# A selective-scan and attention kernel: the C-row product and the state sums of a group placed after the slot's other TensorE work, and y copied and gated one slot later

## The chip, the cores and the metric

One core of one Trainium2 chip. The metric is the device time of one execution in microseconds (us). The engines are named as the profile names them: PE (TensorE matmuls; PEld is its weight loads), DVE (VectorE), ACT (ScalarE), POOL (GpSimd) and SP (SyncE, which issues most DMAs). Each engine works through its own queue in the order in which the kernel's instructions were written down; between engines, semaphores hold an instruction back until what it needs is there.

## The reference

The input x is 4 batches of 512 channels on 64 x 64 positions (4096 tokens a batch), float32. Two residual layers follow each other, each on a group-normed input:

```python
x = x + mamba_layer(group_norm(x))       # layer 0
x = x + linear_attention(group_norm(x))  # layer 1
```

Layer 0 normalizes each token, cuts the 512 channels into 4 chunks of 128 and runs the same selective scan on each chunk, then a norm and a 512 x 512 projection. In a chunk, 128 channels are projected to xi and z of 256 channels each; xi goes through a causal convolution of 4 taps and silu to give xc; from xc come dt (256 channels), B and C (16 states each per token). Then, token after token:

```python
dA = exp(dt_t[:, :, None] * A)                       # 256 channels x 16 states
h  = dA * h + (dt_t * x_t)[:, :, None] * B_t[:, None, :]
y  = einsum('bds,bs->bd', h, C_t)                    # sum over the 16 states
...
y  = (y + xc * D_param) * silu(z)
out = einsum('bld,od->blo', y, out_proj_w)
```

Layer 1 is a linear attention with 8 heads: q, k through relu, k^T q summed over all tokens of a batch, normalized, and then applied to v and the output projection. Its work needs all tokens of layer 0 of a batch, and runs beside layer 0 of the next batch.

## The kernel before

**Tiling.** A step is one batch b, one tile t of 512 tokens and one chunk c of 128 channels: 4 x 8 x 4 = 128 steps. A step has 256 inner channels in two halves e of 128, and 16 states in four quarters q of 4. A pair (e, q) is a *group*: its tile h is 128 x 4 x 512, where the partition holds 4 states x 32 channels and the middle index j one of four blocks of 32 channels. So there are 8 groups a step and 1024 in all. A group takes two *slots* (jj = 0 and 1), each with two of the four j: 16 slots a step, 2048 in all. In what follows an even slot has jj == 0 and an odd slot jj == 1.

**One slot** (`slot`, line 725) writes down, in this order:

- POOL: `drive(g + 2)` (line 717), the product bx = (dt x) B for the slot after next (3 buffers);
- SP: the loads of a row of B (even slots) or of the last 128 columns of C (odd slots), each broadcast over partitions;
- DVE: the first scan (line 739) of 512 tokens, h[j] = dA h + bx, from a dA in PSUM and a bx in SBUF. ACT: the `decay` of number k + 3 (line 708), dA = exp(dt A), into one of three PSUM banks, so it follows scan k;
- in an even slot only, between the first and the second scan, for the group that ended in the slot before: `product(g - 1)` (line 756), in which DVE multiplies the first 384 columns of h by C, read from the PSUM tile c_all; and `fold_states(g - 1)` (line 761), all on PE: `c_row` (line 702) makes the next c_all by a matmul with a selection matrix, at q == 0 four small matmuls put xc D into the y bank (`diagonal`, line 128), and four matmuls with `fold` sum the states of h into y;
- the second scan and its decay;
- in an odd slot, POOL: the last state of each channel is copied to `st`, and the last 128 columns of h are multiplied by C (line 751);
- `after()` (line 1108), everything else.

The tiles h have two buffers, so the first scan of an even slot overwrites the h of the group before last, and waits until its four fold matmuls are done. The c_all tile and the y tile have one bank each. Three more PSUM banks (`ps_w`) serve all other matmuls in turn.

**The rest of the work.** `after()` runs in each slot s = 0..15 of a step n. First the things that are due: a matmul result written to a `ps_w` bank in one slot is copied out, mostly by ACT, one slot later (`later`, line 86). Then, by slot number: `take_y` (line 777), in which ACT copies y from PSUM to SBUF once a half is summed up; `spread` (line 633), 8 DMA issues on SP that load dt and dt x of the next half; `gate` (line 780), in which POOL multiplies y by silu(z); the time steps of step n + 1 (matmuls in slot 2, ACT in slot 3); `out_proj` of step n - 1 in slot 4 (four matmuls on the input, then two on the gated y); the input projection with its convolution for step n + 2 (`inputs`, line 579, `pc` and `pz` banks) in slots 3 to 9; silu in slot 10; the projections to dt, B and C (`mixers`, line 642) from slot 12 on. Last, a planner takes pieces of three queues (the norm of the next tile, the output of a finished tile, the attention of a finished batch) as long as a credit of 3.5 matmuls of 512 columns a slot allows. What has been written down since the slot before, folds included, is charged to that credit.

After the last step, the attention of the last batch runs alone.

Of the kernel before, what the change touches and what calls it, by code (L numbers as in the profile page):

```python
# [24 lines left out]
def kernel(  # L25
# [349 lines left out]
    def bc(v, n):  # L375
        return v.unsqueeze(1).to_broadcast([P, n, v.shape[-1]])
# [256 lines left out]
    def spread(f, e, nm):  # L633

        d = wk.tile([P, 2, NJ, T], F32, tag="d_all", name=f"d_all_{nm}_{e}")
        for v in range(2):
            src = f["d_rows", v].rearrange("(j i) e t -> i e j t", i=BLK)[:, e]
            for k in range(KS):
                nc.sync.dma_start(d[k * BLK : (k + 1) * BLK, v], src)  # L639
        f["d_all", e] = d  # L640
# [33 lines left out]
    SLOTS = NH * NQ * JJ  # L674
    AWAY = (3, 10)

    def place(g):

        n, r = divmod(g, SLOTS)
        e, r = divmod(r, NQ * JJ)  # L680
        return n, e, *divmod(r, JJ)
# [35 lines left out]
    def drive(g):  # L717

        n, e, q, jj = place(g)
        bxs[g] = wk.tile([P, 2, T], F32, tag="bx", name=f"bx_{g}", bufs=3)  # L720
        nc.gpsimd.tensor_tensor(  # L721
            bxs[g], fs[n]["d_all", e][:, 1, jj * 2 : jj * 2 + 2, :], bc(b_all[g // JJ], 2), ALU.mult
        )

    def slot(g, last, after):
        n, e, q, jj = place(g)
        b, t, c = steps[n]
        if g + 2 < last:
            drive(g + 2)
        if jj == 0:  # L730
            if g + 3 * JJ < last:
                b_row(g + 3 * JJ)
            hs[g // JJ] = wk.tile([P, NJ, T], F32, tag="h", name=f"h_{g}", bufs=2)
        elif g + 1 < last:
            c_tail(g + 1)
        h = hs[g // JJ]
        for i in range(2):
            j = jj * 2 + i
            nc.vector.tensor_tensor_scan(  # L739
                h[:, j, :], dAs.pop(2 * g + i), bxs[g][:, i, :],  # L740
                0.0 if t == 0 else st[:, c, e, q, j : j + 1], ALU.mult, ALU.add,
            )
            if 2 * g + i + LEAD < 2 * last:
                decay(2 * g + i + LEAD)
            if i == 0 and jj == 0 and g:
                product(g - 1)
                fold_states(g - 1, last)
        del bxs[g]
        if jj == JJ - 1:
            nc.gpsimd.tensor_copy(st[:, c, e, q, :], h[:, :, T - 1])  # L750
            nc.gpsimd.tensor_tensor(  # L751
                h[:, :, CUT:], h[:, :, CUT:], bc(c_sb.pop(g // JJ), NJ), ALU.mult
            )
        after()

    def product(g):

# [3 lines left out]
    def fold_states(g, last):  # L761

        n, e, q, _ = place(g)
        if g + 1 < last:
            c_row(g + 1)
        if q == 0:
            ys[n, e] = ps_y.tile([P, T], F32, tag="y", name=f"y_{n}_{e}")
            diagonal(ys[n, e], dg[:, e, :], fs[n]["xz"][:, 0, e, :])
        h = hs.pop(g // JJ)
        for j in range(NJ):  # L770
            mm(
                ys[n, e][j * BLK : (j + 1) * BLK, :], fold, h[:, j, :],
                start=False, stop=(q == NQ - 1), abreast=NJ,
            )
# [5 lines left out]
    def gate(f, e):  # L780
        nc.gpsimd.tensor_tensor(  # L781
            f["xz"][:, 1, e, :], f["xz"][:, 1, e, :], f["xz"][:, 0, e, :], ALU.mult
        )
# [224 lines left out]
    names = [f"{b}_{t}_{c}" for b, t, c in steps]  # L1008
# [85 lines left out]
    with tc.manual_schedule():  # L1094
        credit, seen, mix, held[0], held_x[0] = 0.0, work["mm"], iter(()), 0, 0
        for n, (b, t, c) in enumerate(steps):
            f, nm = fs[n], names[n]
            before = fs[n - 1] if n else None
            nxt = fs[n + 1] if n + 1 < N else None
            front = step_inputs(n + 2) if n + 2 < N else iter(())  # L1100
            last_mix, mix = mix, mixers(fs[n + 2], names[n + 2]) if n + 2 < N else iter(())
            if c == 0 and (t + 1 < NT or b + 1 < B):
                add_to(ahead, tile_norm(b, t + 1) if t + 1 < NT else tile_norm(b + 1, 0))
            if c == 0 and t == 0 and b + 1 < B:
                add_to(light, input_norm(b + 1))
            assert c != 2 or not ahead
            for s in range(SLOTS):
                def after():
                    nonlocal credit, seen
                    now[0] = n * SLOTS + s  # L1110
                    for what in [w for at, w in due if at <= now[0]]:
                        what()
                    due[:] = [d for d in due if d[0] > now[0]]
                    if s == 0 and before is not None:
                        take_y(before, n - 1, 1)
                    if s == SLOTS // 2:
                        take_y(f, n, 0)
                    if s < 2:
                        next(last_mix, None)
                    if s == 1:  # L1120
                        spread(f, 1, nm)
                        if before is not None:
                            gate(before, 1)
                    if s == 2 and nxt is not None:
                        time_banks(nxt, names[n + 1])
                    if s == 3 and nxt is not None:
                        nc.scalar.preload_act_table_set("softplus")
                        time_steps(nxt, names[n + 1])
                        nc.scalar.preload_act_table_set("natural_log_exp_and_others")
                    if s == 6 and before is not None:  # L1130
                        pb_, pt_, pc_ = steps[n - 1]
                        with_skip(before, xn[pb_, pt_], pc_)
                        if pc_ == NC - 1:
                            add_to(late, leave(pb_, pt_))
                    if s in (3, 5, 6, 7, 8, 9):
                        next(front, None)
                    if s == 4 and nxt is not None:
                        to_rows(nxt, 0, names[n + 1])
                        to_rows(nxt, 1, names[n + 1])
                    if s == 4 and before is not None:  # L1140
                        pb_, pt_, pc_ = steps[n - 1]
                        out_proj(before, xn[pb_, pt_], pc_, names[n - 1])
                    if s == 9:
                        gate(f, 0)
                        if nxt is not None:
                            spread(nxt, 0, names[n + 1])
                    if s == 10 and n + 2 < N:
                        silu(n + 2)
                        nc.scalar.preload_act_table_set("natural_log_exp_and_others")
                    if s >= 12:  # L1150
                        next(mix, None)
                    may = [
                        what for k, what in ((0, "wide"), (1, "one ahead"), (2, "two ahead"))
                        if any(a - 2 * k <= s <= a - k for a in AWAY) or (k == 2 and s == SLOTS - 1)
                    ]
                    if light and light[0][1] == "wait" or s in AWAY and not any(
                        q and q[0][1] == "wide" for q in (ahead, late)
                    ):
                        one(light)

                    limit[0] = 1 if 0 < s < 6 else 2
                    credit = min(credit + 3.5 - (work["mm"] - seen), 2.6)
                    busy = False
                    for queue in (ahead, late, rest):
                        kind = queue[0][1] if queue else None
                        if queue is ahead or kind == "free" or credit > 0 or kind == "more" and not busy:
                            start = work["mm"]
                            one(queue, ANYWHERE if queue is ahead and (c, s) > (1, 4) else may)
                            credit -= work["mm"] - start
                            busy = busy or work["mm"] - start > 1  # L1170
                    seen = work["mm"]

                slot(n * SLOTS + s, N * SLOTS, after)
            fs[n - 1].clear() if n else None
        product(N * SLOTS - 1)
        fold_states(N * SLOTS - 1, N * SLOTS)
        now[0] = None
        for _, what in due:
            what()
# [60 lines left out]
```

## Time and profile before

| | us |
|---|---|
| median of 3 runs | 7947.08 |
| lowest, highest | 7937.27, 7951.86 |
| the profiled execution's own time | 7963.09 |
| its span, first to last instruction | 7961.4 |
| first scan starts, last scan ends | 122, 7493 |

| engine | busy us of the span | its largest groups (count, mean ns) |
|---|---|---|
| DVE | 6977.7 | scans (4096, 1264 and 1203), product with c_all (1024, 1726) |
| POOL | 6880.5 | bx (2048, 2367), last columns of C (1024, 1270), gate (256, 1272) |
| PE | 6453.6 | fold (8192 records, 696), pc (2048, 645), pq (2048, 604), c_all (1024, 361) |
| ACT | 5507.6 | dA (4096, 687), copies of y (256, 582) |

A busy time is the sum of an engine's instructions in one profiled execution. In a list of waits, a line "A <- B: t, n, m" says that engine and tile A stood idle for t us in all, n times, m at the longest, until B released it. In a time line each row is a start, a duration, the engine, the line and operation, what it writes and reads, how often, and in brackets the idle time before it with its releaser. A float32 matmul shows as two records. The mean granted TensorE clock of the execution was 0.897 of full speed.

### The profile page before, as it was taken

What the parts mean: (1) busy time and instruction counts of PE and PEld (TensorE: products, weight loads), DVE (VectorE), ACT (ScalarE), POOL (GpSimd) and SP (SyncE); (2) the same over time, 40 slices, a digit from 0 to 9 for tenths busy, and PEclk for the clock granted to TensorE, in tenths of its full rate; (3) what the DMA queues carried; (4) which work ended last, traced back from release to release, by engine and by line L of the source; (5) the groups of instructions that cost most, each with busy time, mean ns of one, the idle gap of its engine ahead of it and who ended that gap; (6) DMA issues with size and microseconds to landing.
All of it is one profiled execution on the core that took longest, in us unless ns stands there. A gap on an engine that the chain in (4) does not pass through costs nothing.

```text
span 7961.4 us, 90563 instructions
## 1 busy us (share of the span) xinstructions
PE 6453.6 (81%) x24835; PEld 2120.0 (27%) x24880; DVE 6977.7 (88%) x5766; ACT 5507.6 (69%) x8321; POOL 6880.5 (86%) x4597
## 2 busy tenths in 40 slices
PE   5676777677789888888788888898688888888599
PEld 1121212112223222322222223332122332322144
DVE  5999999999999999989999999998999999988600
ACT  4667777777777777767777777677777777777421
POOL 4999999999999899989999899898999999889600
PEclk7888888888899999998899999899899999999799
DMA  5666666666666666777766666677666666676402
GB/s 154 167 168 166 151 155 159 160 155 167 169 179 162 151 163 159 174 189 175 174 155 171 171 157 161 155 185 189 156 167 163 161 161 159 145 194 180 112 32 90
DMA packets 829184, 1265.87 MB, mean 159 GB/s; under 512 B 183912, under 2 KB 317560, under 8 KB 816384
## 3 DMA queue, kind: packets, MB, share of 16 engines
q1 hardware_dynamic: 804736, 1222.32, 61.1%
q0 software_dynamic: 16896, 33.56, 2.4%
q10 hardware_dynamic: 7040, 4.20, 0.2%
q8 instruction: 195, 3.19, 0.2%
q14 instruction: 317, 2.60, 0.1%
HBM read 1052.78 MB, written 206.57 MB: 158 GB/s over the span
## 4 chain that ended last, share of the span: by engine, by line
DVE 33%; PE 21%; ACT 15%; DMA 12%; issue 8%; SPq 6%; POOL 6%; POOLq 0%; ACTq 0%; DVEq 0%
DVE h L739 22%; DVE h L759 9%; DMA d_all<-d_rows 7%; ACT dA L713 5%; PE pq L124 5%; POOL bx L721 4%; PE pc L124 4%; SPq L688 3%; PE y L124 3%; PE pr L124 3%; SPq L639 2%; DMA c_sb<-c_rows 2%; ACT xz L1048 2%; PE po L124 2%; ACT L1048 1%
## 5 line engine op out<-in xcount | busy, mean ns | idle before, releaser
L721 POOL TENSOR_TENSOR bx<-d_all,b_all 128x1024 f32<-128x1024 f32 x2048 | 4824.7, 2367 | 213.3 <-DVE h L739 195.1
L739 DVE TENSOR_TENSOR_SCAN h<-dA,st,bx 128x512 f32<-128x512 f32 x3584 | 4358.9, 1264 | 358.7 <-ACT dA L713 159.0
L713 ACT ACTIVATE dA<-d_all,a_t 128x512 f32<-128x512 f32 x4096 | 2752.9, 687 | 1568.5 <-DVE h L739 1521.8
L759 DVE TENSOR_TENSOR h<-h,c_all 128x1536 f32<-128x1536 f32 x1024 | 1767.5, 1726 | 0.1
L751 POOL TENSOR_TENSOR h<-h,c_sb 128x512 f32<-128x512 f32 x1024 | 1300.2, 1270 | 190.2 <-DMA c_sb<-c_rows 95.2
L124 PE MATMUL y<-h,fold 128*32 128x512 f32 x8192 | 1271.2, 696 | 71.6 <-POOL h L751 67.4
L124 PE MATMUL c_all<-parts,sel 128*128 128x384 bf16 x1024 | 369.9, 361 | 1123.3 <-DVE h L759 1121.7
L124 PE MATMUL pc<-xn,w_cv 128*128 128x512 f32 x2048 | 1045.7, 645 | 122.8 <-DVE xn L414 62.1
L124 PE MATMUL pq<-w_qk,xa 128*128 128x512 f32 x2048 | 965.5, 604 | 7.9 <-issue 5.3
L739 DVE TENSOR_TENSOR_SCAN h<-dA,bx 128x512 f32<-128x512 f32 x512 | 591.2, 1203 | 90.0 <-ACT dA L713 65.1
L124 PEld LDWEIGHTS <-sel 128*128 128x128 bf16 x1280 | 127.1, 99 | 1762.2 <-DVE h L759 1562.5
L124 PEld LDWEIGHTS pc<-xn,w_cv 128*128 128x128 f32 x2048 | 389.5, 201 | 747.1 <-issue 424.7
L124 PEld LDWEIGHTS pq<-w_qk,xa 128*128 128x128 f32 x2048 | 398.6, 196 | 439.6 <-issue 422.4
L124 PE MATMUL pr<-xb,m 128*128 128x512 f32 x1024 | 485.3, 612 | 7.5 <-DMA xb<-x 3.6
L124 PE MATMUL pp<-xn,w_pr 128*128 128x512 f32 x1024 | 477.7, 597 | 4.8 <-DVE xn L414 4.8
L124 PEld LDWEIGHTS y<-h,fold 128*32 128x32 f32 x8192 | 170.6, 114 | 644.0 <-issue 344.9
L124 PE MATMUL y<-xz,dg 32*32 32x512 f32 x2048 | 337.3, 734 | 0.0
L781 POOL TENSOR_TENSOR xz<-xz 128x512 f32<-128x512 f32 x256 | 325.7, 1272 | 9.2 <-ACT xz L778 9.2
L832 ACT ACTIVATE kq<-pq 128x512 f32<-128x512 f32 x256 | 150.5, 588 | 259.9 <-PE pq L124 259.2
L124 PE MATMUL pd<-xz,w_xp 128*128 128x512 f32 x512 | 323.4, 764 | 7.8 <-ACT xz L1048 7.8
L628 POOL TENSOR_TENSOR dt<-dt,xz 128x1024 f32<-128x1024 f32 x128 | 302.3, 2361 | 24.7 <-ACT dt L620 24.6
L124 PE MATMUL pz<-xn,w_z 128*128 128x512 f32 x512 | 275.4, 631 | 11.7 <-ACT xz L608 8.2
(179 smaller groups left out, 6034.1 us busy)
## 6 DMA issues: line engine op xcount, KB each, us to landing
d_all<-d_rows SPq DMA_DIRECT2D x2048, 256.0 KB, 6.7
b_all<-b_rows SPq DMA_DIRECT2D x4096, 64.0 KB, 2.2
d_rows<-dt SPq DMA_DIRECT2D x256, 512.0 KB, 3.6
c_sb<-c_rows SPq DMA_DIRECT2D x4096, 16.0 KB, 1.8
xs<-in_x_dram SPq DMA_DIRECT2D x32, 1024.0 KB, 6.3
xn<-in_x_dram SPq DMA_DIRECT2D x32, 1024.0 KB, 6.2
xr<-in_x_dram POOLq DMA_DIRECT2D x32, 1024.0 KB, 10.7
x<-xr SPq DMA_DIRECT2D x32, 1024.0 KB, 4.2
```

The costliest lines, as they stand in the source:

```text
L124: nc.tensor.matmul(out_, lhsT, rhs, **how)
L628: nc.gpsimd.tensor_tensor(f["both"][:, 1], f["both"][:, 0], f["xz"][:, 0], ALU.mult)
L639: nc.sync.dma_start(d[k * BLK : (k + 1) * BLK, v], src)
L688: nc.sync.dma_start(dst[k * BLK : (k + 1) * BLK, :], rows_[q * KS + k, :].partition_broadcast(BLK))
L713: nc.scalar.activation(dAs[k], fs[n]["d_all", e][:, 0, j, :], AF.Exp, scale=a_t[:, e, j, q : q + 1])
L721: nc.gpsimd.tensor_tensor(bxs[g], fs[n]["d_all", e][:, 1, jj * 2 : jj * 2 + 2, :], bc(b_all[g // JJ], 2), ALU.mult)
L739: nc.vector.tensor_tensor_scan(h[:, j, :], dAs.pop(2 * g + i), bxs[g][:, i, :], 0.0 if t == 0 else st[:, c, e, q, j : j + 1], ALU.mult, AL ...
L751: nc.gpsimd.tensor_tensor(h[:, :, CUT:], h[:, :, CUT:], bc(c_sb.pop(g // JJ), NJ), ALU.mult)
L759: nc.vector.tensor_tensor(own, own, bc(c_all.pop(g // JJ), NJ), ALU.mult)
L781: nc.gpsimd.tensor_tensor(f["xz"][:, 1, e, :], f["xz"][:, 1, e, :], f["xz"][:, 0, e, :], ALU.mult)
L832: nc.scalar.activation(qk[i], pq, AF.Relu)
L1048: nc.scalar.activation(fs[n]["xz"], fs[n]["xz"], AF.Silu)
```

## The change

Three places move; no computation is added or removed.

1. `fold_states(g - 1)` (the next c_all, the diagonal and the fold matmuls) is written down after `after()` of the even slot, where it stood between the two scans. `product(g - 1)` on DVE stays where it was. On PE, the even slot's other matmuls now stand ahead of c_all and the fold.
2. `take_y` moves from slots 0 and 8 to slots 1 and 9.
3. `gate` moves from slots 1 and 9 to slots 2 and 10; `spread` stays in slots 1 and 9.

```diff
@@ slot
                 decay(2 * g + i + LEAD)
             if i == 0 and jj == 0 and g:
                 product(g - 1)
-                fold_states(g - 1, last)
         del bxs[g]
...
         after()
+        if jj == 0 and g:
+            fold_states(g - 1, last)
@@ after
-                    if s == 0 and before is not None:
+                    if s == 1 and before is not None:
                         take_y(before, n - 1, 1)
-                    if s == SLOTS // 2:
+                    if s == SLOTS // 2 + 1:
                         take_y(f, n, 0)
                     if s < 2:
                         next(last_mix, None)
                     if s == 1:
                         spread(f, 1, nm)
-                        if before is not None:
-                            gate(before, 1)
+                    if s == 2 and before is not None:
+                        gate(before, 1)
...
-                    if s == 9:
+                    if s == 9 and nxt is not None:
+                        spread(nxt, 0, names[n + 1])
+                    if s == 10:
                         gate(f, 0)
-                        if nxt is not None:
-                            spread(nxt, 0, names[n + 1])
```

Since the fold of a group is now written down behind the planner's piece of its slot, the planner counts it towards the odd slot that follows.

## The prediction

> **What bounds the kernel now.** I read the busy table and the slices of the page first, then the waits inside the scan loop (122 to 7493 us after the start, the first scan to the last), then one step of the time line.
>
> ```profile
> PE 6453.6 (81%) x24835; PEld 2120.0 (27%) x24880; DVE 6977.7 (88%) x5766; ACT 5507.6 (69%) x8321; POOL 6880.5 (86%) x4597
> ...
> L739 DVE TENSOR_TENSOR_SCAN h<-dA,st,bx 128x512 f32<-128x512 f32 x3584 | 4358.9, 1264 | 358.7 <-ACT dA L713 159.0
> L759 DVE TENSOR_TENSOR h<-h,c_all 128x1536 f32<-128x1536 f32 x1024 | 1767.5, 1726 | 0.1
> ```
>
> VectorE sets the pace. In the loop's 7371 us it is busy for 6913 (the loop as one window), so all its idle time there is 458 us; no reordering of other engines can win more. A group (two slots, four scans at 1.26 us and one product at 1.73) is 6.8 us of VectorE alone, and a group takes 7371/1024 = 7.2 us. The loop's other waits:
>
> ```profile
> PEld L124 <- DVE h L759: 1562.5, 664, 10.5
> ACT dA L713 <- DVE h L739: 1521.8, 1482, 11.1
> PE c_all L124 <- DVE h L759: 1121.7, 477, 10.4
> ...
> DVE h L739 <- ACT dA L713: 224.0, 186, 46.4
> ...
> DVE h L739 <- PE y L124: 90.8, 88, 3.9
> ACT xz L778 <- PE y L124: 85.1, 93, 3.4
> DVE h L739 <- POOL bx L721: 78.0, 70, 4.7
> ```
>
> TensorE stands 664 times, 2.35 us each, in front of the weights of a c_all, waiting for the product. That is the wait the change moves work into. ScalarE's largest wait is for scans: decay number k+3 reuses the bank of decay k, so in every slot ScalarE's second decay starts only after the slot's second scan, and every PSUM copy of that slot stands behind it. The 88 waits of scans for y are scans that need an h buffer whose fold was late. Now slot 6 of one step (its product ends at 4020.17):
>
> ```profile
> 4020.09 4.80 DVE L739 TENSOR_TENSOR_SCAN h<-dA,st,bx 128x512 f32<-128x512 f32 x4
> 4020.23 0.34 PE L124 MATMUL c_all<-parts,sel 128*128 128x384 bf16 x1 [0.56 <-DVE h L759]
> 4020.49 1.07 PE L124 MATMUL y<-h,fold 128*32 128x512 f32 x8
> 4021.40 0.69 ACT L713 ACTIVATE dA<-d_all,a_t 128x512 f32<-128x512 f32 x1 [1.50 <-DVE h L739]
> ...
> 4022.03 0.67 ACT L592 ACTIVATE xz<-pc,cb 128x512 f32<-128x512 f32 x1
> ...
> 4022.75 3.70 PE L124 MATMUL pc<-xn,w_cv 128*128 128x512 f32 x8 [1.19 <-ACT xz L592]
> ```
>
> The reader is to see the order. TensorE folds at once after the product (done at 4021.56) and then stands 1.19 us for a copy that is behind the decay of scan two. The four scans end at 4024.89, 1.2 us apart; the fourth is slot 8's first, which overwrites the h buffer just folded, and it could start at 4023.65. Today the fold has 2.1 us to spare.
>
> **The change, part by part.** Instruction counts do not change. "Even" is the work of a slot with jj == 0, "odd" that of the next.
>
> *The fold behind the slot's products.* c_all and fold take 4021.56 - 4020.23 = 1.33 us from the first start; with the four diagonal matmuls (slots 2 and 10) 1.0 more, 2.33. They now stand behind the even slot's matmuls. Those that wait for nothing late fill the 2.35 us wait. Those that wait for a PSUM copy of the same slot can't: they start at scan two's end + decay + copy, and the fold follows them. In the example: 4022.75, four records of pc (two matmuls, 1.95 us by the row's 3.70 for eight and its neighbours) to 4024.70, and 1.33 to 4026.03, where the scan could start at 4023.65: 2.4 us late, on the engine that sets the end. What is late next is the whole chain, since scan, product, decays and bx all follow that scan.
>
> How often: from the order in which the changed program's instructions stand on each engine, and the semaphore count each waits for, I counted the even slots in which a matmul ahead of the fold waits for ScalarE work that stands behind the slot's second decay. They are 244 of 1021. The lateness is chain (decay 0.69 plus the copies, at 0.58 to 0.68 from their rows) + matmuls from that wait to the fold (0.97 us each of 512 columns, 0.25 where four stand abreast) + fold - two scans (2.5) - other VectorE work there (0.3; after slot 2 1.4, after slot 10 0.9, as xn's subtraction and scaling at 2.26 us stand there in one step of four):
>
> - slot 6: 97 times, 1.84 + 1.97 + 1.33 - 2.8 = 2.34, in all 227 us (the front's second pc bank waits for the copy of its first; three banks)
> - slot 8: 36 x 1.85 = 67; slot 12: 41 x 1.40 = 57; slot 10: 17 x 2.07 = 35
> - slot 4: 19 x 1.41 = 27; slot 0: 8 x 2.97 = 24; slot 2: 26 x 0.82 = 21; slot 14: none
>
> Sum 458 us. Slot 4 is late for another reason too: between its fold and the one before stand 6.45 us of matmuls (2.67 odd, 3.78 even; out_proj is there) where 4.45 stood. From the instruction times of this trace its fold ends 2.96 us after the product on the mean and the next scan could start 4.36 after: 2.0 later is 0.6 past that, on the other 109 steps 65 us. Elsewhere these sums hardly differ between the two orders.
>
> Bounds: below, 0 (the copies come so much earlier that the wait is gone; nothing in the rows shows it, as the decay ahead of them waits for scan two in any order); above, 721, the sum over all groups of the later of both reasons, each group's lateness set against this trace's own scan times with no relief for TensorE from the delay before. I take 458 + 65.
>
> *What it wins.* The 91 us of scans waiting for y are the same place, and are in the new price: minus 91. ACT xz<-y (85) goes, since take_y now comes a slot after its fold; the even slot's other copies (res 74, kq 65, xr 56, got_var 39 us of waits for PE in the loop) come sooner. They matter only through the scans' waits for decays and bx: 224 less the single one of 46.4, plus 78, is 256. Bounds 0 and 256; I take 100, as ScalarE's waits for PE, some 320 us, are a fifth of its 1522 for scans.
>
> *c_all later*: its reader is the product two slots on, behind a scan that waits for the later fold anyway: nothing. Without that cover it would delay a product by part of 0.34 us.
>
> *take_y and gate a slot later.* One ScalarE copy (0.58) and one GpSimd multiply (1.27), 256 of each, moved past one slot's decays and one bx (2.37); no DMA moves, and the SP queue keeps its order (spread stays at slot 9). The y bank is wanted again by the diagonal at slot 2's end, a slot (3.6 us) after the copy. Readers of the gate: out_proj in slot 4; in the step shown the gate ends at 4004.07 and out_proj's product with it starts at 4014.97, 10.9 us, of which a slot and the 2.4 us of an earlier TensorE leave some 5. Cost nothing; with that cover gone, TensorE would stand at out_proj with slot 4's fold queued behind it.
>
> *The planner.* Fold and c_all are now charged to the odd slot's credit, so optional matmuls move to even slots. That is inside the counts.
>
> Sum: 458 + 65 - 91 - 100 = +332. The profiled execution took 7963.1 (span 7961.4): 8295. It lies 16 above the median of 7947.1, so the forecast is **8280 us**.
>
> *The clock.* Granted clock is 0.82 from 122 to 1000 us, where TensorE waits most, and 0.92 after 5000. The Trainium skill ("TensorE: Matmul & The Clock Gate", section "Why this matters for your kernels") says to leave no idle gap over about 3 us between bursts, as the clock then falls to half. By it, filling the wait for the product would bring the clock towards 1; a tenth off the 3 us of matmul and fold in each of 244 late groups is an estimate of 73 us less, 8207. By the rows the wait only changes place, to behind the even slot's first half, and I leave the clock as it is.
>
> **The rivals.**
>
> *Faster (0.18).* Even matmuls end before the product does, folds start as now, and the copies gain. For it: 664 waits of 2.35 us, and the even work is 2.1 us on the mean. Against it: slot 6 above. It gives 91 and a third of the decays' 178, so 7947 - 150 = 7797. It decides if waits behind the second decay are hit in fewer than some 80 groups (150/1.9).
>
> *TensorE becomes the second bound (0.12).* A late fold delays odd matmuls, their copies, and the next fold, with no relief: 7947 + 721 - 91 = 8577. For it: TensorE is busy 5968 of 7371 us of the loop. Against it: a delayed scan gives TensorE the same time back.
>
> *The gains cancel the price (0.05)*: 80 groups late, 7947.
>
> *The charge to another slot is all that matters (0.03)*: folds late in slot 4 only, 7947 + 65 = 8012.
>
> **How the numbers follow.** The likeliest has 0.62 and its own range is 8080 to 8520 (price of 523 between two thirds, 349, with gains of 216, and four thirds, 697, with gains of 124). The 8 in 10 range takes in the two outer rivals, **7790 to 8620**. About 0.2% is what a measurement of this kernel can tell from no change. Slower: 0.62 + 0.12 + 0.03 + 0.01 = 0.78; same 0.03; faster 0.19.
>
> **What would show it.** Right: scans waiting for PE y go from 91 us (88 times) to about 500 (over 240 times), most at slot 8's first scan; in slot 6 pc stands ahead of c_all and both behind xz<-pc; ACT xz<-y falls from 85 to near nothing; PE's wait for the product falls below 600 us. Wrong: scans wait for y no longer than now, or the loop's VectorE idle time falls under 458 us; or scans come to wait for decays instead; or PE stands at out_proj for the gate.

## The result, and the profile after

The changed kernel takes 8837.92 us (median of 4 runs, 8828.76 to 8842.6) where the kernel before takes 7945.64 beside it: 892 us more, a ratio of 1.1119 with a 95% interval of 1.1102 to 1.1136. The forecast was 8280, and its range ended at 8620. The direction and the place were right. The size was not: the scans that come late were more, and later, than the forecast summed up.

First the busy line and three groups of the page of the changed kernel, in the columns of the page before (busy time, mean ns of one, idle time before it and its releaser):

```profile
PE 7038.8 (80%) x24880; PEld 2215.6 (25%) x24880; DVE 6984.9 (79%) x5766; ACT 5528.5 (63%) x8321; POOL 6900.5 (78%) x4597
...
L739 DVE TENSOR_TENSOR_SCAN h<-dA,st,bx 128x512 f32<-128x512 f32 x3584 | 4370.9, 1265 | 1215.0 <-PE y L124 952.8
...
L760 DVE TENSOR_TENSOR h<-h,c_all 128x1536 f32<-128x1536 f32 x1024 | 1768.0, 1727 | 0.1
...
L124 PE MATMUL c_all<-parts,sel 128*128 128x384 bf16 x1024 | 383.1, 374 | 384.9 <-DVE h L760 384.3
```

VectorE does the same work (6985 us against 6978). What grew is its idle time ahead of scans: 1215 us where 359 stood, nearly all of it for the fold (y on PE). The list of what VectorE waited for, in the whole span:

```profile
DVE h L739 <- PE y L124: 1003.8, 377, 7.2
DVE kq L840 <- PE pk L124: 235.5, 33, 7.6
DVE h L739 <- ACT dA L713: 169.7, 122, 49.4
DVE h L739 <- POOL bx L721: 116.8, 43, 5.1
```

The wait for y went from 91 us (88 times) to 1004 (377 times, 2.7 us each): 913 more, as much as the whole loss of 892. The waits for decays and for bx, 302 us together before, are still 287.

Now what TensorE waited for:

```profile
PE c_all L124 <- DVE h L760: 384.3, 240, 10.0
PE pc L124 <- ACT xz L592: 218.2, 84, 4.5
PE pd L124 <- ACT parts L664: 135.6, 85, 4.0
PE pd L124 <- ACT xz L1049: 121.6, 72, 3.9
PE pd L124 <- ACT parts L669: 108.9, 65, 3.4
PE pt L124 <- ACT kq L833: 69.6, 37, 2.7
PE pt L124 <- ACT parts L669: 64.0, 37, 4.5
```

The wait for the product shrank from 1122 us to 384. But in its place stand waits for copies and silu on ACT. Three of these lines in the list of the kernel before (the silu is line 1048 there):

```profile
PE pc L124 <- ACT xz L592: 23.4, 22, 2.4
PE pd L124 <- ACT xz L1048: 7.8, 2, 3.9
PE pd L124 <- ACT parts L664: 3.7, 8, 1.1
```

Summed over all matmul lines, TensorE's waits for VectorE fell from 1235 to 559 us, and those for ACT rose from 157 to 1181. The work was moved into a wait for the product and met other waits there, and the fold now stands behind them.

A step's slots 4 to 6 in the time line of the changed kernel (start, duration, engine, operation, idle before it):

```profile
1207.74 0.33 PE L124 MATMUL c_all<-parts,sel 128*128 128x384 bf16 x1
1207.99 1.06 PE L124 MATMUL y<-h,fold 128*32 128x512 f32 x8
...
1209.23 1.28 DVE L739 TENSOR_TENSOR_SCAN h<-dA,st,bx 128x512 f32<-128x512 f32 x1 [1.67 <-PE y L124]
...
1212.07 3.62 DVE L739 TENSOR_TENSOR_SCAN h<-dA,st,bx 128x512 f32<-128x512 f32 x3
1213.38 0.69 ACT L713 ACTIVATE dA<-d_all,a_t 128x512 f32<-128x512 f32 x1 [2.15 <-DVE h L739]
1214.01 0.67 ACT L592 ACTIVATE xz<-pc,cb 128x512 f32<-128x512 f32 x1
...
1214.73 3.51 PE L124 MATMUL pc<-xn,w_cv 128*128 128x512 f32 x4 [2.04 <-ACT xz L592]
...
1218.03 2.10 PE L124 MATMUL pp<-xn,w_pr 128*128 128x512 f32 x4
1219.97 0.33 PE L124 MATMUL c_all<-parts,sel 128*128 128x384 bf16 x1
1220.22 1.06 PE L124 MATMUL y<-h,fold 128*32 128x512 f32 x8
...
1221.45 1.28 DVE L739 TENSOR_TENSOR_SCAN h<-dA,st,bx 128x512 f32<-128x512 f32 x1 [5.75 <-PE y L124]
```

It is the chain that the forecast drew: second scan, decay, copy of the first pc bank, second pc bank, fold, first scan of slot 8. It starts as drawn: 1.38 us from the second scan's end, 1213.35, to pc, and 1.39 in the rows of the kernel before. Two things were not drawn. The four records of pc take 3.51 us, where 1.95 was costed: TensorE had just stood idle for 2.04 us, and the clock records show half clock from 1215.04 to 1218.46. And a piece of the planner (pp, 2.1 us) stands between pc and the fold in this step. The scan is 5.75 us late. In the step before there is no such piece, and pc runs at full clock although the idle time ahead of it was longer:

```profile
1155.50 1.99 PE L124 MATMUL pc<-xn,w_cv 128*128 128x512 f32 x4 [2.90 <-ACT xz L592]
...
1158.81 1.28 DVE L739 TENSOR_TENSOR_SCAN h<-dA,st,bx 128x512 f32<-128x512 f32 x1 [2.34 <-PE y L124]
```

There the scan is 2.34 us late, as the forecast had it.

By the slot in which the fold stands, the idle time of the next group's first scan, worked out from the instruction times of both traces (us in all, whatever released the scan; for y alone the sums are 91 and 1004):

| fold in slot | 0 | 2 | 4 | 6 | 8 | 10 | 12 | 14 | sum |
|---|---|---|---|---|---|---|---|---|---|
| before | 1 | 20 | 23 | 100 | 25 | 47 | 1 | 13 | 230 |
| after | 92 | 175 | 199 | 373 | 105 | 86 | 136 | 19 | 1185 |
| forecast, as a price | 24 | 21 | 92 | 227 | 67 | 35 | 57 | 0 | 523 |

### The profile page after: what moved, and what is told of

The parts are those of the page before. It is cut to its first block, busy times and chain, and to the rows that moved or that the text cites. A ratio compares the mean times of both kernels' runs of the same rounds, so it can differ in the third digit from the quotient of the medians.

```text
span 8839.2 us, 90768 instructions
## 1 busy us (share of the span) xinstructions
PE 7038.8 (80%) x24880; PEld 2215.6 (25%) x24880; DVE 6984.9 (79%) x5766; ACT 5528.5 (63%) x8321; POOL 6900.5 (78%) x4597
## 4 chain that ended last, share of the span: by engine, by line
DVE 37%; PE 28%; ACT 15%; issue 10%; DMA 5%; POOL 3%; SPq 2%; DVEq 0%; POOLq 0%; ACTq 0%; another core or an unknown queue 0%
DVE h L739 22%; DVE h L760 13%; PE pq L124 6%; PE y L124 6%; PE pc L124 4%; ACT dA L713 4%; PE pr L124 3%; POOL bx L721 2%; PE po L124 2%; DMA d_all<-d_rows 2%; ACT xz L1049 2%; ACT L1049 1%; SPq L688 1%; ACT L1150 1%; PE pp L124 1%
## 5 line engine op out<-in xcount | busy, mean ns | idle before, releaser
L124 PE MATMUL pc<-xn,w_cv 128*128 128x512 f32 x2048 | 1121.0, 677 | 283.5 <-ACT xz L592 218.2
L124 PE MATMUL y<-h,fold 128*32 128x512 f32 x8192 | 1305.6, 713 | 13.2 <-POOL h L750 10.0
L124 PE MATMUL pq<-w_qk,xa 128*128 128x512 f32 x2048 | 1042.9, 640 | 5.1 <-ACT xa L367 5.1
L124 PE MATMUL pr<-xb,m 128*128 128x512 f32 x1024 | 520.5, 645 | 85.6 <-ACT res L980 45.8
L124 PE MATMUL pp<-xn,w_pr 128*128 128x512 f32 x1024 | 498.8, 616 | 29.2 <-ACT xz L608 13.2
L124 PE MATMUL pt<-dt,w_dt 32*128 32x512 f32 x512 | 328.0, 863 | 157.5 <-ACT kq L833 69.6
L124 PE MATMUL y<-xz,dg 32*32 32x512 f32 x2048 | 390.0, 842 | 0.0
L124 PE MATMUL pz<-xn,w_z 128*128 128x512 f32 x512 | 296.2, 662 | 28.7 <-ACT xz L592 27.8
```

Of the source, the lines that this page charges most:

```text
L124: nc.tensor.matmul(out_, lhsT, rhs, **how)
```

## The experiments

Each was timed beside the kernel before on one chip, and its ratio is to those runs (medians from 7943 to 7959 us). "After" is the changed kernel's 8838 us, timed beside 7946; differences against it are good to some 15 us.

**E1: y later alone.** The fold goes back between the scans; `take_y` and `gate` stay a slot later.

```diff
             if i == 0 and jj == 0 and g:
                 product(g - 1)
+                fold_states(g - 1, last)
...
         after()
-        if jj == 0 and g:
-            fold_states(g - 1, last)
```

> The changed kernel with the fold back between the two scans; take_y and gate stay one slot later. Theory 1 (the price is the fold behind the even slot's other matmuls): 7946 within 16 us, the copy and the gate a slot later cost nothing. Rival (the later y or gate holds TensorE at the diagonal or at out_proj): 100 us or more above 7946, with TensorE waiting for POOL xz or ACT xz.

Measured: 7951.31 us, ratio 1.0005 (0.9995 to 1.0014). The later copy and gate cost nothing, so the whole loss belongs to the place of the fold.

**E2: three h buffers, after the change.**

```diff
...
-            hs[g // JJ] = wk.tile([P, NJ, T], F32, tag="h", name=f"h_{g}", bufs=2)
+            hs[g // JJ] = wk.tile([P, NJ, T], F32, tag="h", name=f"h_{g}", bufs=3)
...
-    w_qk = const_rows(wqk, "w_qk")
+    w_qk = const_rows(wqk[:, 0:C], "w_qk")
...
-                        pq, gn[:, c, u * P : (u + 1) * P], w_qk[:, c, j * C : (j + 1) * C],
+                        pq, gn[:, c, u * P : (u + 1) * P], w_qk[:, c, 0:C],
```

> The changed kernel with three h buffers for two, so that a late fold does not hold the next group's first scan. To make room k is computed with q's weights (half of w_qk is kept), same instructions and sizes. Theory 1 (the price is scans that wait for the h buffer): most of the 890 us come back, 7900 to 8150, scans waiting for PE y below 200 us. Rival (TensorE or the copies behind it have become a second bound): 8500 or more, the wait moves to scans for decays, or to the product for c_all.

Measured: 8046.96 us, ratio 1.0126 (1.0109 to 1.0143). 791 of the 887 us that the change costs beside the same runs of before come back. VectorE's waits in it:

```profile
DVE h L760 <- PE c_all L124: 273.6, 166, 7.9
DVE kq L840 <- PE pk L124: 249.3, 43, 7.6
DVE h L739 <- ACT dA L713: 244.1, 145, 49.0
```

No line of scans that wait for y is left among the large ones. So most of the loss passes through the h buffer, and TensorE's throughput is not the limit: it does the same work in 8047 us. The largest wait that is new is the next thing behind the same work, the product that waits for its c_all (0.1 us of idle before the change).

**E3: the charge of the fold.** `cost` is the fold's and c_all's credit; it is charged ahead of `after()` and taken off again behind the fold.

```diff
                 product(g - 1)
+                work["mm"] += cost(g - 1, last)
...
             fold_states(g - 1, last)
+            work["mm"] -= cost(g - 1, last)
```

> The changed kernel with fold and c_all charged to the even slot's credit, as before the change, and still written down last in the slot. Theory 1 (fixed work and late inputs of the even slots): 8650 to 8840. Rival (the planner's pieces that moved to even slots ahead of the fold are the larger part of the price): below 8450.

Measured: 8834.28 us, ratio 1.1112 (1.1096 to 1.1129). Where the planner books the fold changes nothing that can be told from noise.

**E4: the fold between the slot's fixed work and the planner's pieces.**

```diff
...
-        after()
-        if jj == 0 and g:
-            fold_states(g - 1, last)
+        fold_now[0] = g - 1 if jj == 0 and g else None
+        after()
...
+                    if fold_now[0] is not None:
+                        fold_states(fold_now[0], N * SLOTS)
+
                     limit[0] = 1 if 0 < s < 6 else 2
```

> The changed kernel with fold and c_all written down in after(), behind the slot's fixed work and ahead of the planner's pieces (charged to the even slot). Theory 1: the pieces behind the fold no longer delay it, the fixed work (pt in slot 2, out_proj in 4, pc in 6, pd in 12) still does: 8250 to 8500, slot 6's lateness stays. Rival (planner's pieces are all of it): below 8050. Rival (they are none of it): above 8700.

Measured: 8234.29 us, ratio 1.036 (1.0344 to 1.0375). With the planner's pieces behind the fold 604 us of the loss come back, a little more than was expected, and 283 are left with the fixed work ahead of it. Its waits for y are

```profile
DVE h L740 <- PE y L124: 421.1, 199, 5.9
```

By slot, counted as in the table above, 406 of 506 us are left in 4 (160, out_proj) and 6 (246, pc).

**E5 and E6: the due copies ahead of the second decay.** Everything that is due in a slot is written down ahead of the slot's second decay, in the changed kernel (E5) and in the kernel before (E6).

```diff
+                if i == 1:
+                    copies(g)
                 decay(2 * g + i + LEAD)
...
+    def copies(s):
+        now[0] = s
+        for what in [w for at, w in due if at <= s]:
+            what()
+        due[:] = [d for d in due if d[0] > s]
```

> The changed kernel with the copies that are due in a slot written down ahead of the slot's second decay instead of behind it (in every slot; everything else that is due moves with them). Theory 1b (the even slot's matmuls cannot start in the wait for the product, since their inputs and banks hang on copies that stand behind a decay that waits for a scan): copies end about 1.2 us sooner, 150 to 450 us of the 890 come back, 8390 to 8690, TensorE's waits for pc, pd and pt on ACT shrink. Rival (it is the mere amount of matmul work between product and fold): 8750 or more.

> The kernel before with the same move of the copies. Theory 1b: TensorE's fold stands ahead of the work that waits for copies, so little comes of it: 7900 to 7970. Rival (second decays pushed behind copies cost scans): above 8000, scans waiting for ACT dA above 400 us.

Measured: E5 8242.14 us, ratio 1.0374 (1.0358 to 1.0389); E6 7944.8, ratio 0.9998 (0.9988 to 1.0007). Not a matmul was taken out from between product and fold in E5, and still 596 of the 895 us came back, more than was expected. VectorE's waits in E5:

```profile
DVE h L739 <- PE y L124: 381.5, 225, 7.1
DVE kq L848 <- PE pk L124: 247.6, 43, 7.6
DVE h L739 <- ACT dA L713: 213.7, 141, 8.0
```

TensorE's waits for ACT, summed over its matmul lines, fall from 1181 to 688 us. By slot, the gain is in 6, whose pc waits for a copy (late scans fall from 373 to 81 us), in 8 (105 to 14), in 2 (175 to 89), in 10 (86 to 29) and in 0 (92 to 45). Slot 4, where hardly a matmul waits for such a copy, stays (199 and 202). In the kernel before the same move does nothing, since there the fold stands ahead of all that waits for copies.

**E7 and E8: some slots only.** The fold goes back between the scans in the slots EARLY, (6,) in E7 and (2, 4, 6, 8, 12) in E8.

```diff
                 product(g - 1)
+                if g % SLOTS in EARLY:
+                    fold_states(g - 1, last)
...
-        if jj == 0 and g:
+        if jj == 0 and g and g % SLOTS not in EARLY:
             fold_states(g - 1, last)
```

> The changed kernel with fold and c_all of slot 6 alone back between the scans. If each slot pays its own lateness: 273 us back (scan 8's wait falls from 373 to 100), 8560. If slot 6 inherits its lateness from slot 4's late fold, it stays late in its old place too: scan 8's wait stays above 200 us and 8650 or more. If a late slot 6 also made 8 to 12 late: below 8480.

> The fold behind the slot's work in slots 0, 10 and 14 alone, back between the scans in 2, 4, 6, 8 and 12. Theory 1: the price of the three slots as read in the changed kernel's trace, 92 + 86 + 19 less the 61 there before, so 8050 to 8110. Rival (the three slots are late only because the heavy ones before them were): 7940 to 7970. Rival (where the fold can wait, the earlier matmuls win): below 7930.

Measured: E7 8530.15 us, ratio 1.074 (1.0722 to 1.0759); E8 8217.12, ratio 1.0341 (1.0326 to 1.0356). E7 gives back 308 us, where 273 were expected: slot 6's lateness falls from 373 to 14 us, further than was thought, but slot 8's rises from 105 to 156. E8 costs 274 us, twice what was expected of its three slots. Slots 10 and 14, each behind a slot with an early fold, are the reason: 173 and 61 us, against the 86 and 19 that they had with all folds late; slot 0, behind a late one, has 81 for 92. Between an early fold and a late one stand the even matmuls of both slots (8 and 10, say) and the odd ones between; only where both folds have the same place is it one even slot. A mixed order pays for each switch from early to late.

**E9: three h buffers, before the change** (the edit of E2 on the kernel before).

> The kernel before with three h buffers; k is computed with q's weights to make room, as in the other run with three buffers. It says what the wait for the h buffer was worth before the change, and what of 8047 with three buffers after it is left to explain. Theory 1: the 91 us of scans that wait for y go, 7850 to 7900, and the change with three buffers then costs 150 to 200 us, which its scans do not show as waits for y but as products that wait for c_all. Rival (a scan released sooner only waits for its decay or bx instead): 7930 to 7960, 90 to 110 us left.

Measured: 7915.64 us, ratio 0.9944 (0.9929 to 0.9959), so less came of it than expected. The 91 us of waits for y are gone from its lists, but those for decays are 317 us where 224 stood, as the rival had it:

```profile
DVE h L739 <- ACT dA L713: 316.7, 205, 48.3
```

The time lies between the two expectations. With three buffers in both, the change still costs 1.8% (1.0126 over 0.9944), some 145 us of the kernel before's time.

**E10: both remedies** (E4 and E5 together, on the changed kernel).

> The changed kernel with both remedies: fold ahead of the planner's pieces, and the due copies ahead of the slot's second decay. If the two causes (pieces ahead of the fold; matmuls that wait for copies) were separate, 604 and 596 us would come back together and more than the 888 lost; so they overlap. Theory 1b: slot 4's 4.4 us of matmuls that wait for nothing stay, 150 to 200 us: 8050 to 8150. Rival (the remedies are the same one twice): 8200 or more.

Measured: 8063.39 us, ratio 1.0132 (1.0115 to 1.0149). The two remedies overlap: together they give back 775 us, not 1200. Of the 271 us of waits for y that are left, slot 4 has 153.

## Why the prediction was right, and where it was wrong

**The place was right.** Scans wait for y, most at slot 8's first scan; E1 and E2 show that it is the fold, and the h buffer through which it acts. Of the 244 groups counted in the instruction order as bound by a copy of the same slot, 242 were late by over 0.3 us in the trace. Slot 4 is late for a second reason, as forecast, and resists both remedies.

**What was missed.** Summed by group, the late scans after the change are 1187 us where 523 were priced: 795 for 458 in the counted groups, and 392 for 65 in the others. 230 us of the 1187 were there before, of which only the 91 for y were taken off; of the 100 us taken off for gains, 15 came.

**The step that failed first: "Those that wait for nothing late fill the 2.35 us wait."** The other 776 groups of the table were priced at 65 us, all in slot 4. In the trace 202 of them are late, for 392 us: 152 in slot 4, 78 in slot 2, 53 in slot 0, 46 in slot 10 (slot 10 had 47 before the change too). The count asked which even matmuls wait for ACT work behind the decay of their own slot. It left out all that stands in an odd slot or waits for work written down earlier; before the change most of these waits lay beside the wait for the product and did not show, though the program's order names them. The wait to be filled was also smaller than it was read: the 664 waits are those of the weight load, which overlaps other matmuls; TensorE itself stood 477 times, 1122 us in all. In slot 2, 58 of the 78 us stand in groups whose longest wait is that of the time-step matmuls (pt) for their bank. In slot 0, 46 of 53 us stand behind matmuls that wait for VectorE's addition to kq (line 840), which the count, made for ACT, could not find. Not every new wait costs something: pd waits for some 360 us in slots 12, 14 and 0, but only 62 of them are ahead of a late scan, and slot 14, which has 136 of them, is late by 19.

**The second: the lateness of a bound group, 1.88 us.** This term missed by 337 us, the one before by 327. It was 3.26 on the mean, 795 us for 458. In 218 of these groups the trace shows TensorE idle for ACT work behind the decay. There the stretch from the second scan's end to c_all took 4.03 us, where the forecast's terms give 3.33; from c_all to the fold's end it took 1.88, for 1.51; the scan started 0.17 after that, which was not costed; and VectorE's own work meanwhile, taken off at 2.96, took 2.77. A third of that time the clock stood at half. The planner's pieces count as well: in slot 6 the 52 groups with pc alone behind the wait were 3.02 us late, the 28 with pp or pq behind it too 5.2. That the half clock causes its part is read from the records; no run took it away by itself. E5, which moves copies and leaves TensorE's order as it is, gives back 596 us, most of it in slots 6 and 8, where the counted groups are. E4 gives back as much by other means, and E10 shows that the two overlap.

**The third: slot 4.** 2.0 us more work against 1.4 us of mean room was priced as 0.6 us on each group. A scan can't gain from a group with room to spare, so the late ones count by themselves: 176 us more than before, for 92. In the trace 90 of 128 are late. In 43 of them, late by 2.9 us each (126 us), the pc of slot 3 first waits for VectorE's xn (line 414), 1.28 us on the mean; in 39, late by 1.5 us each (60 us), no matmul between the folds waits for more than 0.15 us.

**The gains were too large.** 100 us were taken for scans that wait less for decays and bx; 15 came (302 to 287). ACT's copy of y, forecast to stop waiting for PE, did not: its line has 116.9 us over the span, where 93.6 stood. The 91 us of waits for y were rightly netted against the new ones.

**What cost nothing did cost nothing**, the y copy, the gate and the planner's charge (E1, E3). c_all later is hidden behind the wait for the fold, as said. But its price without that cover was put at part of 0.34 us a group; E2 takes the cover away, and it is 274 us, 166 times 1.6 us, as c_all too stands behind all of the slot's matmuls.

**The rivals.** TensorE as a second bound, at 8577, was nearest and for the wrong reason: with a third h buffer it does all its work in 8047 us. The argument against it, that a delayed scan gives TensorE the time back, did not hold either: of the 878 us by which the profiled span grew, TensorE was busy for 585 more with the same matmuls (6453.6 to 7038.8), and its waits for VectorE and ACT together grew by 348 (1392 to 1740). The faster case fell with the first step.

**The clock went the other way.** The mean granted clock fell from 0.897 to 0.863, and the time at half clock rose from 1642 to 2417 us in the clock records. The estimate drawn from the Trainium skill ("TensorE: Matmul & The Clock Gate", section "Why this matters for your kernels") took the wait to be filled; the idle time was only moved, as the forecast itself had said. The page's figure for the idle gap, about 3 us, is not the bound seen here: pc was slow (3.51 us) after 2.04 us of idle time, and at full clock (1.99 us) after 2.90 us in the step before.

## What to carry to other kernels

A matmul whose result releases a buffer of the engine that sets the pace belongs at the head of its queue, even if its engine waits for it: here its distance from that wait is the price. Work fits into a wait only if its own inputs are there when the wait begins; ask of every wait it has, for whichever engine, also those that stand beside the old wait and so do not show in the profile, when it ends, and whether its slot has room for it. And lateness is to be summed group by group, as positive parts: in slot 4 a mean of room against a mean of work hid half of it.

## What the runs showed of the hardware

An idle gap of TensorE of 2 to 3 us is often, but not always, followed by half clock. The scan loop of the changed kernel has 249 such gaps with full clock in the microsecond ahead of them; in 188 the clock records have half clock within the next 2 us. Of 164 gaps of 1 to 2 us it is 42. In the kernel before it is 70 of 90 and 8 of 165.

Records of pc and pq (128 x 512 float32) that start at full clock take 0.61 us on the mean, those that start at half clock 1.03; 5.8% of them started at half clock before the change and 12.2% after it. E4 and E10 have the clock of the kernel before again (0.896 and 0.894). E5, as fast as E4, has 0.883: the granted clock alone does not set the time.
